# Reordering the borders of a two-pass gated-experts kernel: turnings and row loads ahead in the first unit, forms of the second pass made early, results copied out by ScalarE, residual rows loaded ahead

## The chip, the cores and the metric

The kernel runs on one core of one Trainium2 chip. The metric is device time in microseconds (us) of one execution; smaller is better. A core has TensorE (PE, with its weight loads as PEld), VectorE (DVE), ScalarE (ACT), GpSimd (POOL) and SyncE (SP), which issues nearly all DMAs here.

## The reference

Nine gated feed-forward networks (eight experts and a shared one) run on every token, their outputs are weighted and summed, and the input is added. The arrays are `x` (8, 512, 256), the gates (8, 8), the shared gate (8), and per network two weights of 256 x 1024 and one of 1024 x 256, all float32.

```python
g = einsum('bsd,edf->ebsf', h, Wg)
u = einsum('bsd,edf->ebsf', h, Wu)
expert_outs = einsum('ebsf,efd->ebsd', silu(g) * u, Wd)
expert_output = einsum('be,ebsd->bsd', gating_probs, expert_outs)
shared = einsum('bsf,fd->bsd', silu(h @ Sg) * (h @ Su), Sd)
sg = shared_gate_prob[:, :, None]
x + (1.0 - sg) * expert_output + sg * shared
```

## The kernel before

**Passes and units.** The eight batch rows are worked in two passes of four (`NH` = 2, `NI` = 4). In a pass, each of the nine networks is worked in two groups of 512 of its 1024 columns, so a pass has 18 units and the kernel 36. The last unit of a pass `closes` it, the first one `opens` it.

**Fewer products.** A unit needs the product of four weight blocks with four batch rows, for the gate (m = 0) and the up projection (m = 1). It doesn't compute all of them plainly. With a number `CI[i]` per row (0, 1, -1, 2), the two halves of a turned row and of a weight block are combined: `P_step` and `Q_step` make the four products of a block with its own row, and for each of six pairs (i, j) `R1_step` multiplies a difference of weights U by a difference of rows V and `R_step` sums of weights W by sums of rows b. `P_step` reads the half `xhub[h, i][:, 0]`, `Q_step` the half `[:, 1]`. Every product streams 512 columns.

**Forms of the rows.** For a pair, V (one 128 x 512 tile) and b (two of them) depend on the pass alone. In the unit that opens a pass they are computed, V by VectorE (`x_difference`, L169, with a ScalarE multiply L171 where needed), b by VectorE (L183) and GpSimd (L184), and stored to a DRAM scratch `xs` (L188, L189). The other 17 units load them from there (L173, L191).

**Turnings.** `turn_x` loads a batch row in two DMAs (`load_rows`), turns it with TensorE transposes (L128), and copies the two halves out by ScalarE (L150) and VectorE (L152, L154). In the first unit this happens between the products; for the second pass it happens in the last unit of the first.

**Weights.** `load_w` loads a block's weights in two DMAs (L226), `make_at` combines them by GpSimd, and for `CI` = 2 with a ScalarE multiply first (L243, L244). The next unit's weights are loaded in the steps of pairs 2 to 5.

**Down projection.** `down` multiplies the unit before by its third weight, seven products of two for each of two row pairs, into two PSUM banks `po0` and `po1` that take turns. Sums that persist over a pass are in `acc`. In the last unit of a pass the results are finished, and `ends` lists the blocks to be written.

**Results.** `turn_back` loads the residual rows `xr` (L441), turns the block into a PSUM bank (L128, named `pto`), adds with VectorE from PSUM (L448), and stores to `out` (L449). In the first unit of pass two it takes the next `po` bank, and `turned` notes that this bank is not seeded afterwards. At the end of the kernel it takes a gate bank.

**Order.** TensorE and GpSimd keep the program's order (`manual_schedule`); the instructions of VectorE, ScalarE and SP are ordered by the scheduler of the framework, by their place in the program among those that it reckons ready. A tile's buffer comes free after its last use; a tile that finds no free buffer of its tag makes its writer wait. The string `ORDER` mixes the steps of `gate_up` (G) with those of `down` (D). In unit 0, D stands for two turnings of `turn_x`; in other units for a `turn_back`, if one is listed, and a step of `down`.

## Time and profile before

| what | us |
|---|---|
| three runs | 2537.35, 2539.17, 2541.19 |
| median | 2539.17 |
| the profiled execution | 2537.59 |
| its span, first to last instruction | 2535.6 |

The span is what the profile shows; the execution's own time holds about 2 us more around it. Busy time is the union of an engine's records. A TensorE record lasts longer than the distance to the next (0.59 against 0.43 us), so TensorE's pace is read from the starts of its matmuls. A logical float32 product appears as two matmuls of 128 x 512, a transposition of one 128 x 512 half as four of 128 x 128. Unit 0 takes the time to about 70 us, and the first unit of pass two begins near 1240 us.

### The profile page before, as it was taken

Reading aid. Unit: us, or ns where it says so; the run is one execution under the profiler, and the core shown is the slowest. Engines: PE = TensorE matmul, PEld = TensorE weight load, DVE = VectorE, ACT = ScalarE, POOL = GpSimd, SP = SyncE. Lnnn points to the kernel's source line nnn. Section 1 sums busy time; section 2 is a strip of 40 time slices with the busy share of each in tenths; the row PEclk is TensorE's granted clock in tenths of the full one; section 3 lists DMA queues with packets and bytes.
Section 4 is the critical chain, followed back from the end, with each engine's and each line's share of the span. In section 5 each row is a group of like instructions: output and inputs, shape, how many; then the busy total and the mean of one; then the engine's idle time right before and its main releaser. Section 6 shows DMA issues by size and latency. Waiting matters only on the chain.

```text
span 2535.6 us, 22085 instructions
## 1 busy us (share of the span) xinstructions
PE 2502.4 (99%) x5896; PEld 1110.6 (44%) x5896; DVE 1499.3 (59%) x2267; ACT 1140.2 (45%) x2072; POOL 1908.7 (75%) x2062
## 2 busy tenths in 40 slices
PE   8999999999999999999989999999999999999998
PEld 3444444444444444444434444444444444444443
DVE  7655555555555555555785555555555555555556
ACT  3344444444444444444323444444444444444443
POOL 6778777777777777877677777877777778777773
PEclk9999999999999999999999999999999999999999
DMA  5322323233332322323343322322323333233222
GB/s 169 97 81 92 89 92 92 87 100 96 100 93 90 100 87 81 93 88 96 108 142 103 99 88 81 90 91 91 92 87 100 96 100 92 91 99 88 82 72 79
DMA packets 179738, 240.57 MB, mean 95 GB/s; under 512 B 13728, under 2 KB 122272, under 8 KB 179616
## 3 DMA queue, kind: packets, MB, share of 16 engines
q1 hardware_dynamic: 179328, 239.13, 30.8%
q8 instruction: 49, 0.80, 0.1%
q14 instruction: 73, 0.60, 0.1%
q10 hardware_dynamic: 288, 0.04, 0.0%
HBM read 225.48 MB, written 13.63 MB: 94 GB/s over the span
## 4 chain that ended last, share of the span: by engine, by line
PE 96%; DVE 2%; DMA 1%; issue 1%; POOL 0%; ACT 0%; SPq 0%; DVEq 0%; ACTq 0%; POOLq 0%
PE po L409 33%; PE c L363 29%; PE c L353 14%; PE c L309 10%; PE c L340 10%; DMA xr<-in_x_dram 0%; DVE h L300 0%; PE ptx L128 0%; DMA out_dram<-xr 0%; DVE xr L448 0%; DVE c L358 0%; DMA xin<-in_x_dram 0%; POOL z L325 0%; DMA w<-in_L_cond_Wu_dram 0%; DVE b L183 0%
## 5 line engine op out<-in xcount | busy, mean ns | idle before, releaser
L363 PE MATMUL c<-b,wb 128*128 128x512 f32 x1728 | 816.4, 594 | 1.0 <-POOL wb L244 1.0
L325 POOL TENSOR_TENSOR z<-P,Q 128x512 f32<-128x512 f32 x432 | 542.3, 1286 | 121.8 <-DVE Q L346 75.2
L300 DVE SCALAR_TENSOR_TENSOR h<-sg,coef,c 128x512 f32<-128x512 f32 x576 | 427.2, 742 | 231.5 <-PE c L363 221.8
L424 ACT COPY acc<-po 128x512 f32<-128x512 f32 x476 | 278.3, 585 | 582.9 <-PE po L409 580.0
L294 ACT ACTIVATE sg<-c 128x512 f32<-128x512 f32 x576 | 341.9, 595 | 378.7 <-PE c L363 206.3
L363 PEld LDWEIGHTS c<-b,wb 128*128 128x128 f32 x1728 | 328.9, 191 | 412.4 <-issue 393.1
L382 POOL TENSOR_TENSOR T<-h,h 128x512 f32<-128x512 f32 x284 | 357.5, 1277 | 116.1 <-PE po L409 71.9
L409 PE MATMUL po<-T,sd 128*128 128x512 f32 x864 | 435.1, 593 | 1.7 <-DVE xr L448 1.1
L353 PE MATMUL c<-v,u 128*128 128x512 f32 x864 | 435.7, 593 | 0.9 <-DVE Q L346 0.7
L357 DVE TENSOR_TENSOR c<-z,c 128x512 f32<-128x512 f32 x288 | 200.0, 695 | 335.2 <-ACT sg L294 264.1
L382 POOL TENSOR_TENSOR T<-h,T 128x512 f32<-128x512 f32 x284 | 355.8, 1277 | 6.9 <-PE po L409 6.9
L368 DVE TENSOR_TENSOR c<-c,Q 128x512 f32<-128x512 f32 x288 | 200.5, 698 | 186.5 <-PE c L363 186.5
L244 POOL TENSOR_TENSOR wb<-wb,u 128x256 f32<-128x256 f32 x216 | 155.0, 743 | 206.7 <-ACT wb L243 206.7
L409 PE MATMUL po<-h,wd 128*128 128x512 f32 x576 | 293.7, 593 | 2.0 <-DVE xr L448 2.0
L400 ACT COPY po<-acc 128x512 f32<-128x512 f32 x464 | 273.9, 590 | 43.2 <-DVE acc L426 17.0
L309 PE MATMUL c<-x,w 128*128 128x512 f32 x576 | 279.5, 598 | 7.0 <-DVE x L154 3.2
L346 DVE TENSOR_TENSOR Q<-c,P 128x512 f32<-128x512 f32 x288 | 198.1, 688 | 112.6 <-ACT sg L294 112.3
L353 PEld LDWEIGHTS c<-v,u 128*128 128x128 f32 x864 | 164.2, 190 | 208.1 <-issue 190.1
L409 PEld LDWEIGHTS po<-T,sd 128*128 128x128 f32 x864 | 163.6, 190 | 207.1 <-issue 185.9
L313 ACT COPY P<-c 128x512 f32<-128x512 f32 x288 | 168.0, 584 | 136.8 <-PE c L309 136.7
L340 PE MATMUL c<-x,at 128*128 128x512 f32 x432 | 203.0, 592 | 0.0
L358 DVE TENSOR_TENSOR c<-c,z 128x512 f32<-128x512 f32 x288 | 199.5, 693 | 0.0
(60 smaller groups left out, 1863.7 us busy)
## 6 DMA issues: line engine op xcount, KB each, us to landing
b<-xs SPq DMA_DIRECT2D x204, 512.0 KB, 3.6
v<-xs SPq DMA_DIRECT2D x204, 256.0 KB, 2.6
w<-in_L_cond_Wg_dram SPq DMA_DIRECT2D x128, 128.0 KB, 3.4
w<-in_L_cond_Wu_dram SPq DMA_DIRECT2D x128, 128.0 KB, 3.4
wd<-in_L_cond_Wd_dram SPq DMA_DIRECT2D x64, 256.0 KB, 2.7
xs<-b SPq DMA_DIRECT2D x12, 512.0 KB, 2.8
xin<-in_x_dram SPq DMA_DIRECT2D x16, 256.0 KB, 3.9
xr<-in_x_dram SPq DMA_DIRECT2D x16, 256.0 KB, 3.2
```

Source lines behind the costliest of these rows:

```text
L294: nc.scalar.activation(s, bank, AF.Silu)
L300: ve.scalar_tensor_tensor(t, u.sg[i, j], coef[:, u.e, b : b + 1], bank, ALU.mult, ALU.mult)
L309: nc.tensor.matmul(bank, u.raw[i][:, m, 0], xhub[u.h, i][:, 0], start=True, stop=True)
L325: gp.tensor_tensor(z, u.Ps[i, m], u.Qs[o, m], ALU.add)
L340: nc.tensor.matmul(bank, u.at[i][:, m], xhub[u.h, i][:, 1], start=False, stop=True, skip_group_check=True,)
L353: nc.tensor.matmul(bank, u.U[p][:, m], u.V[p], start=True, stop=True)
L363: nc.tensor.matmul(bank, u.W[p][:, r, m], u.VB[p][:, r], start=False, stop=True, skip_group_check=True,)
L368: ve.tensor_add(bank, bank, u.Qs[j, m])
L382: eng.tensor_tensor(t, a, b, ALU.subtract)
L400: nc.scalar.copy(po, acc[J, x])
L409: nc.tensor.matmul(po, u.wd[I][x], b, start=first, stop=True, skip_group_check=not first,)
L424: nc.scalar.copy(acc[J, x], po)
```

## The change

- *Unit 0*: all rows and weights are asked for before the first turning, and `make_at` follows the first products. A turning stands one step earlier in the order (`FIRST`). For the row with `CI` = 0 the half `[:, 0]` is turned first. One tiny Silu is put ahead of all ScalarE work. Of the sums z, those of pair 0 go from VectorE to GpSimd, and the combination for `CI` = 2 is two GpSimd sums.
- *Forms of pass two*: for pairs 0, 1 and 2 they are computed and stored in the last unit of pass one (`make_forms`, at its G steps 42, 45 and 48), in tiles of the pool z. The unit that opens pass two loads these three from the scratch.
- *Stores*: where a unit computes forms, their stores are collected and issued in the step of the next pair, after the next unit's `load_w` (`store_forms`).
- *Results of pass one*: ScalarE copies the turned block from PSUM to a tile `to` (one buffer), GpSimd adds the residual rows. The residual rows of a result are loaded when the one before it is written, those of the first as `down` of the closing unit begins (`load_back`).
- *Results of pass two*: all eight residual blocks are loaded before the last `down`, six into tiles of the pool z, two into `io`. The add stays with VectorE.

```diff
--- before.py
+++ after.py
@@ -109,6 +109,7 @@
         ve.tensor_copy(coef[:, E, :], sgt)
 
     scratch = {}
+    back = {}
     xhub = {}
 
 
@@ -137,14 +138,14 @@
             rows.append(t)
         return rows
 
-    def turn_x(h, pool, tag):
-
-        rows = load_rows(pool, tag, NI * h)
+    def turn_x(h, pool, tag, loaded=None):
+
+        rows = loaded or [load_rows(pool, tag, NI * h)]
         for i in range(NI):
             xt = xpool.tile([P, 2, S], F32, tag="x", name=f"x{h}_{i}")
-            for k in (1, 0):
+            for n_, k in enumerate((0, 1) if CI[i] == 0.0 else (1, 0)):
                 pt, n = new_po(f"ptx{h}_{i}_{k}", h > 0)
-                turn(pt, [rows[t // 2][:, t % 2, ts(k, P)] for t in range(NT)])
+                turn(pt, [rows[i][t // 2][:, t % 2, ts(k, P)] for t in range(NT)])
                 turned[n] = True
                 if k == 1:
                     nc.scalar.copy(xt[:, 1], pt)
@@ -154,17 +155,33 @@
                     ve.scalar_tensor_tensor(
                         xt[:, 0], xt[:, 1], -CI[i], pt, ALU.mult, ALU.add
                     )
-                if k == 0:
+                if n_ == 1:
                     xhub[h, i] = xt
-                    if i + 1 < NI:
-                        rows = load_rows(pool, tag, NI * h + i + 1)
+                    if len(rows) < NI:
+                        rows.append(load_rows(pool, tag, NI * h + i + 1))
                 yield
+
+    def make_forms(h, p):
+
+        i, j = PAIRS[p]
+        d = CI[i] - CI[j]
+        v, b0, b1 = (
+            zpool.tile([P, S], F32, tag="z", name=f"f{k}{h}_{p}") for k in range(3)
+        )
+        ve.tensor_sub(v, xhub[h, i][:, 0], xhub[h, j][:, 0])
+        if d != 1.0:
+            nc.scalar.mul(v, v, 1.0 / d)
+        ve.tensor_add(b0, v, xhub[h, j][:, 1])
+        gp.tensor_tensor(b1, v, xhub[h, i][:, 1], ALU.add)
+        scratch[h, p] = dram.tile([P, 3, S], F32, tag=f"xs{h}_{p}", name=f"xs{h}_{p}")
+        for k, t in enumerate((v, b0, b1)):
+            nc.sync.dma_start(scratch[h, p][:, k], t)
 
     def x_difference(u, p):
 
         i, j = PAIRS[p]
         v = vpool.tile([P, S], F32, tag="v", name=f"v{u.name}_{p}")
-        if u.opens:
+        if (u.h, p) not in scratch:
             d = CI[i] - CI[j]
             ve.tensor_sub(v, xhub[u.h, i][:, 0], xhub[u.h, j][:, 0])
             if d != 1.0:
@@ -179,17 +196,22 @@
         i, j = PAIRS[p]
         v = u.V[p]
         b = bpool.tile([P, 2, S], F32, tag="b", name=f"b{u.name}_{p}")
-        if u.opens:
+        if (u.h, p) not in scratch:
             ve.tensor_add(b[:, 0], v, xhub[u.h, j][:, 1])
             gp.tensor_tensor(b[:, 1], v, xhub[u.h, i][:, 1], ALU.add)
             scratch[u.h, p] = dram.tile(
                 [P, 3, S], F32, tag=f"xs{u.h}_{p}", name=f"xs{u.h}_{p}"
             )
-            nc.sync.dma_start(scratch[u.h, p][:, 0], v)
-            nc.sync.dma_start(scratch[u.h, p][:, 1:3], b)
+            u.store.append((scratch[u.h, p], v, b))
         else:
             nc.sync.dma_start(b, scratch[u.h, p][:, 1:3])
         u.VB[p] = b
+
+    def store_forms(u):
+        for to, v, b in u.store:
+            nc.sync.dma_start(to[:, 0], v)
+            nc.sync.dma_start(to[:, 1:3], b)
+        u.store = []
 
     def touch_banks():
 
@@ -198,8 +220,10 @@
             for pool, tag, n in ((ps_g, "g0", 3), (ps_g, "g1", 3), (ps_o, "po0", 1), (ps_o, "po1", 1))
             for k in range(n)
         ]
-        zero = const.tile([P, S], mybir.dt.bfloat16, name="zero")
+        zero = zpool.tile([P, 2 * S], mybir.dt.bfloat16, tag="z", name="zero")[:, :S]
         ve.memset(zero, 0.0)
+        warm = const.tile([P, 1], F32, name="warm")
+        nc.scalar.activation(warm, ident[:, 0:1], AF.Silu)
         for bank in banks:
             nc.tensor.matmul(bank, zero[:, 0:P], zero, start=True, stop=True)
 
@@ -217,7 +241,7 @@
                 u.name = f"{h}_{e}_{g}"
                 u.raw, u.at, u.U, u.W, u.V, u.VB = {}, {}, {}, {}, {}, {}
                 u.Ps, u.Qs, u.z, u.bank, u.h_ = {}, {}, {}, {}, {}
-                u.wd, u.T, u.sg = {}, {}, {}
+                u.wd, u.T, u.sg, u.store = {}, {}, {}, []
                 units.append(u)
 
     def load_w(u, i):
@@ -249,6 +273,11 @@
             u.at[i] = raw[:, :, 1]
             return
         t = atpool.tile([P, 2, P], F32, tag="at", name=f"at{u.name}_{i}")
+        if u.n == 0 and CI[i] == 2.0:
+            gp.tensor_tensor(t, raw[:, :, 0], raw[:, :, 1], ALU.add)
+            gp.tensor_tensor(t, t, raw[:, :, 0], ALU.add)
+            u.at[i] = t
+            return
         scaled_sum(t, CI[i], raw[:, :, 0], raw[:, :, 1], False)
         u.at[i] = t
 
@@ -315,7 +344,7 @@
         for p in range(ZBANK):
             a, b = PAIRS[p]
             if max(a, b) == i:
-                new_z(u, p, m, i, bank)
+                new_z(u, p, m, i, bank if u.n or p else None)
 
     def new_z(u, p, m, i, bank=None):
 
@@ -433,20 +462,39 @@
                     r, c, i = {2: (0, 0, 2), 3: (0, 1, 3), 7: (1, 1, 5), 4: (1, 0, 4)}[x]
                     ends.append((u.h, J, r, c, acc[J, i]))
 
+    BACK = [(J, r, c) for J in range(2) for r, c in ((0, 0), (0, 1), (1, 1), (1, 0))]
+
+    def block_of(a, b, r):
+        return a[b].rearrange("(p t) d -> p t d", t=NT)[:, :, ts(r, P)]
+
+    def load_back(h, J, r, c, pool=None, tag="io"):
+        if (h, J, r, c) not in back:
+            b = NI * h + 2 * J + c
+            xr = (pool or iopool).tile([P, NT, P], F32, tag=tag, name=f"xr{b}_{r}")
+            nc.sync.dma_start(xr, block_of(x, b, r))
+            back[h, J, r, c] = xr
+        return back[h, J, r, c]
+
     def turn_back(h, J, r, c, block):
 
         b = NI * h + 2 * J + c
-        rows = [a[b].rearrange("(p t) d -> p t d", t=NT)[:, :, ts(r, P)] for a in (x, out)]
-        xr = iopool.tile([P, NT, P], F32, tag="io", name=f"xr{b}_{r}")
-        nc.sync.dma_start(xr, rows[0])
+        xr = load_back(h, J, r, c)
         if h + 1 < NH:
             pt, n = new_po(f"pto{b}_{r}", True)
             turned[n] = True
         else:
             pt = ps_g.tile([P, S], F32, tag=f"g{r}", name=f"pto{b}_{r}")
         turn(pt, [block[:, ts(t, P)] for t in range(NT)])
-        ve.tensor_add(xr, pt.rearrange("p (t d) -> p t d", t=NT), xr)
-        nc.sync.dma_start(rows[1], xr)
+        if h + 1 < NH:
+            t = iopool.tile([P, S], F32, tag="to", name=f"to{b}_{r}", bufs=1)
+            nc.scalar.copy(t, pt)
+            gp.tensor_tensor(xr, t.rearrange("p (t d) -> p t d", t=NT), xr, ALU.add)
+        else:
+            ve.tensor_add(xr, pt.rearrange("p (t d) -> p t d", t=NT), xr)
+        nc.sync.dma_start(block_of(out, b, r), xr)
+        n = BACK.index((J, r, c)) + 1
+        if h + 1 < NH and n < len(BACK):
+            load_back(h, *BACK[n])
 
     def gate_up(u, nxt):
 
@@ -490,6 +538,7 @@
                 if p >= 2:
                     load_w(nxt, p - 2)
                     make_at(nxt, p - 2)
+            store_forms(u)
             for m in range(2):
                 if not last:
                     R1_step(u, p + 1, m)
@@ -510,21 +559,23 @@
     HUB = "GGDGGDGGGGDGGGGDGGDDGGDD"
     BLOCKS = ("GDGGDGGGD", "GDGGDGGGD", "GDGGDGDGGD", "GDGGDGGGD", "GDGGDGGGD", "GDGGDGDGGD")
     ORDER = HUB + "".join(BLOCKS)
+    FIRST = "DGGDGGDGG" + "G" * 46
 
 
     ends = []
     with tc.manual_schedule(engines={mybir.EngineType.PE, mybir.EngineType.Pool}):
         touch_banks()
-        turning = turn_x(0, tpool, "t")
-        next(turning)
-        load_w(units[0], 0)
-        make_at(units[0], 0)
-        next(turning)
-        for i in range(1, NI):
+        loaded = []
+        for i in range(NI):
+            loaded.append(load_rows(tpool, "t", i))
             load_w(units[0], i)
-            make_at(units[0], i)
+        turning = turn_x(0, tpool, "t", loaded)
+        for _ in range(2):
+            next(turning)
         for m in range(2):
             P_step(units[0], 0, m)
+        for i in range(NI):
+            make_at(units[0], i)
         make_coef()
         behind, acc = iter(()), {}
         for u in units:
@@ -532,7 +583,7 @@
             nxt = units[u.n + 1] if u.n + 1 < len(units) else None
             g = gate_up(u, nxt)
             nG = 0
-            for what in ORDER:
+            for what in ORDER if u.n else FIRST:
                 if what == "G":
                     if nG == 4 and u.n:
                         for _ in behind:
@@ -542,11 +593,15 @@
                         if pv.opens:
                             acc = {}
                         behind = down(pv, acc, pv.closes)
+                        if pv.closes:
+                            load_back(pv.h, *BACK[0])
                     if final and nxt is not None:
                         if nG == 18:
                             turning = turn_x(u.h + 1, iopool, "io")
                         if nG >= 18 and nG % 3 == 0:
                             next(turning, None)
+                        if nG in (42, 45, 48):
+                            make_forms(u.h + 1, nG // 3 - 14)
                     next(g)
                     nG += 1
                     if nxt is None and nG in (18, 24, 30, 36, 42):
@@ -567,6 +622,8 @@
         pv = units[-1]
         load_d(pv, (1,))
         step, due = 0, []
+        for n, at in enumerate(BACK):
+            load_back(NH - 1, *at, *((zpool, "z") if n < 6 else (iopool, "io")))
         for _ in down(pv, acc, True):
             step += 1
             if due and due[0] < step:
```

## The prediction

> **What bounds the kernel now.** I read the page first, then busy time by stage, then TensorE's waits, then the order of instructions around each wait.
>
> ```profile
> span 2535.6 us, 22085 instructions
> ...
> PE 2502.4 (99%) x5896; PEld 1110.6 (44%) x5896; DVE 1499.3 (59%) x2267; ACT 1140.2 (45%) x2072; POOL 1908.7 (75%) x2062
> ```
>
> TensorE is the bound, but 99% flatters it, since records overlap. In the 1,000 us from 1400 on, 2,331 matmuls give 0.429 us each; all 5,760 of that size need 2,471 us and the 128 transposes (four in 0.43 us) 14. Of the span about 50 us is therefore not matmul work, and all that can be won lies there.
>
> ```profile
> core 0: us, PE busy (x) PEld busy (x) DVE busy (x) ACT busy (x) POOL busy (x), PEclk, DMA share, GB/s
> 0.00:30.00 30.00, 23.83 (x69) 11.16 (x70) 15.28 (x33) 11.15 (x18) 13.22 (x20) 1.00 0.61 194
> 30.00:62.00 32.00, 29.77 (x68) 12.30 (x66) 29.29 (x41) 9.56 (x19) 29.29 (x27) 1.00 0.41 140
> 62.00:70.00 8.00, 5.20 (x9) 2.44 (x10) 5.71 (x10) 1.98 (x5) 5.99 (x9) 0.79 0.58 199
> 1255.00:1278.00 23.00, 23.00 (x61) 10.51 (x60) 18.19 (x24) 7.47 (x14) 23.00 (x19) 1.00 0.24 81
> 1278.00:1300.00 22.00, 16.10 (x38) 6.90 (x37) 16.73 (x22) 3.02 (x6) 18.14 (x17) 0.84 0.34 107
> ...
> 1100.00:1169.00 69.00, 69.00 (x162) 30.54 (x161) 39.94 (x61) 32.82 (x60) 52.91 (x59) 1.00 0.30 92
> ...
> 2526.00:2536.00 10.00, 0.00 (x0) 0.00 (x0) 1.38 (x2) 0.00 (x0) 0.00 (x0) 0.64 0.34 93
> ```
>
> The columns are length, busy time (count) per engine, then granted clock, DMA share, GB/s. The middle of a pass (1100:1169) is full. The gaps are in the first unit (30:62: VectorE 29.29 and GpSimd 29.29 of 32 us; 62:70 at clock 0.79), in the first unit of pass two (1278:1300: 16.10 of 22 us at clock 0.84, and just before it GpSimd at 23.00 of 23.00) and after the last transpose. The waits:
>
> ```profile
> PE po L409 <- DVE xr L448: 9.6, 4, 4.8
> PE c L309 <- DVE x L154: 3.2, 2, 2.0
> PE c L309 <- ACT sg L294: 3.1, 1, 3.1
> ```
>
> I set each row's start beside count times 0.429 us. Up to 30 us TensorE loses after its first product 0.37 + 2.21 + 1.30 us beside small change; from 30 to 60 us 2.6; then this:
>
> ```profile
> 59.82 1.88 PE L363 MATMUL c<-b,wb 128*128 128x512 f32 x4
> 64.80 2.07 PE L309 MATMUL c<-x,w 128*128 128x512 f32 x2 [3.10 <-ACT sg L294]
> ...
> 1278.75 1.02 PE L353 MATMUL c<-v,u 128*128 128x512 f32 x2
> 1284.58 2.05 PE L409 MATMUL po<-T,wd 128*128 128x512 f32 x2 [4.81 <-DVE xr L448]
> ```
>
> The first pair: four products need 1.72 us, so TensorE stands for 3.26 us, and the next rows at half clock cost 1.01 + 0.55. Total 4.82. The second pair: 4.97 of standing, 0.98 + 1.66 of half clock; with later waits of the same name (1.25, 1.78, 2.20) and 0.3 of small change behind them 13.1 us in all.
>
> **The change, part by part.** All sums are against the profiled execution (2537.59 us: span 2535.6 and 2.0 around it), which lies 1.6 under the median of 2539.17; the difference is taken over to the median.
>
> *(1) First turnings.* The half that `P_step` reads is now turned and copied first: ScalarE's copy of the first half starts at 7.21, VectorE's of the second at 8.06, so the first product can start 0.8 us earlier. Turning 1 moves ahead of Q0, 2 ahead of P1, 3 ahead of P2. From turning to finished operand takes 2.0 us (turned by 15.7, VectorE done at 17.7); Q0 (four products, 1.72) and the next turning (0.87) now cover it, so 2.21 and 1.30 go. No TensorE instruction is added. Loads: all eight row and eight weight DMAs go on SP's queue together, about 0.47 us of issue each. Row set 3 needs a buffer of set 0 (turned by 8.04), and weight 3 queues behind it. At the 310 GB/s of 5:10, 3 MB are in by about 12 us; weight 3 lands about 1 us later than now, and GpSimd's `make_at(3)` (two adds of 0.72 in place of ScalarE's multiply and one add) ends near 14.5 instead of 12.86. GpSimd was idle for 5.7 us before 26.01, which hides this and the two sums of 1.28 that `new_z` moves to it; without that cover they cost 4.
>
> *The activation table.* The second load goes:
>
> ```profile
> 13.23 1.28 ACT L294 ACT_TABLE_LOAD   x1
> ...
> 63.36 0.42 ACT L243 ACTIVATE at<-w 128x256 f32<-128x256 f32 x1 [5.99 <-DMA w<-in_L_cond_Wu_dram]
> 63.68 1.06 ACT L294 ACTIVATE sg<-c 128x512 f32<-128x512 f32 x2
> ```
>
> The copy before it ends at 13.21, the first Silu starts at 14.52: 1.3 us. [...]
>
> What of this reaches the end? VectorE is busy almost without a break from 15.15 to 59, so the opening cannot be shortened by more than VectorE is. It starts 1.25 earlier, has two sums less (1.3), and the 1.1 us it idled for ScalarE's copies before the old sums goes: 3.65. Bounds: 1.5 (GpSimd takes the lead) to 6 (the first four products took 3.79 us in place of 1.72, at half clock; an earlier start may end that sooner).
>
> *(2) Stores after loads.* Stores of v and b are issued by `store_forms`, after `load_w`:
>
> ```profile
> 57.37 0.42 SPq L189 DMA_DIRECT2D xs<-b  x1
> ...
> 59.15 0.52 SPq L226 DMA_DIRECT2D w<-in_L_cond_Wu_dram  x1
> ```
>
> The store at 57.37 waits for GpSimd's b, and the weight load at 59.15 stands behind it and the v load. ScalarE waits for this weight at 63.36, two activations queue behind (fence above), and TensorE behind them. The weight's buffer is free after ScalarE's multiply at 57.37; issued then, it is done issuing at 58.3, lands at 61.7 (3.4 us is the median), and TensorE goes on near 63.0 instead of 64.80, 1.5 us after its last product and without half clock. Gain 3.3. Between 0 (SP's order is a scheduler's, stores may stay ahead) and 4.8. Late next: v's buffers, held until the store; the store takes 2.0 us to land and a pair lasts 8, so nothing.
>
> *(3) Forms of pass two early.* For three pairs six VectorE operations, one ScalarE multiply, three GpSimd adds (3.8 us) and nine stores (three more than for these pairs now, 0.33 each on SP) move to the end of pass one. GpSimd idles there 7.0 + 2.5 + 1.3 us between 1218 and 1238; cost 0, without that cover 3.8. In return, SP fetches v and b for these pairs (two loads each), as in every other unit. GpSimd's two adds at 1246 and its 4.0 us wait at 1252 for a weight, whose DMA stood behind the stores of b, should go: it starts its long run about 2 us earlier.
>
> *(4) Results.* Eight VectorE adds (0.68) become eight ScalarE copies (0.59, the row of L424) and eight GpSimd adds (1.28, the row of L325). The bank is freed by the copy. In 1278:1300 ScalarE is busy 3.02 of 22 us, while VectorE reached the add for the transposes of 1277.40 only at 1283.76. So the 13.1 us lose their cause. But GpSimd gets 8 x 1.28 = 10.2 us and loses 3.8; a middle unit has 52.91 of 69. I followed its queue: its run ended in a middle unit 38.9 us after the unit's first difference; here the third form's chain, two result adds and one b come to it, some 2 us of stretching beside VectorE too, so that the second result's add ends near 1286.6. `to` has one buffer: the third copy (transposes at 1282.2 without the old stalls) waits behind that add, and TensorE needs the bank at 1284.3. That is a new stall of 0 to 5 us; I take 2.5. Gain 10.6, bounds 7 and 13. Behind a waiting copy stand ScalarE's activations, behind a waiting add GpSimd's sums. Each residual load is issued one result ahead (3.2 us to land, results 4.7 us apart or more), so the add should rarely wait for it.
>
> [...]
>
> *(5) Last results.* All eight residual blocks are loaded before the last `down`.
>
> ```profile
> 2531.34 0.69 DVE L448 TENSOR_TENSOR xr<-pto,xr 128x512 f32<-128x512 f32 x1 [4.06 <-DMA xr<-in_x_dram]
> 2532.06 0.53 SPq L449 DMA_DIRECT2D out_dram<-xr  x1
> ```
>
> The last transposes end at 2525.5. With the block there, the add runs at 2525.55 instead of 2531.34: 5.8 us. TensorE's wait of 1.1 at 2517 (VectorE stood 1.63 for a block) goes too. Eight loads (2 MB, 0.55 us of SP each) run beside matmuls with the DMAs at 0.31. Gain 6.9, bounds 5 and 8.
>
> Sum: 3.65 + 3.3 + 10.6 + 6.9 = 24.5 us; 2539.2 - 24.5 = 2514.7.
>
> **The rivals.** *GpSimd takes over in pass two's first unit*: only half of part 4 comes (5), total 19, 2520. For it: 23.00 of 23.00. Against: three idle stretches of 2.4, 5.8 and 4.3 us behind it. *It doesn't do what it says at the opening*: VectorE and GpSimd stay the pace and SP keeps stores ahead; 1.5 + 0 + 10.6 + 6.9 = 19, also 2520. *Slower*: the single `to` buffer and GpSimd's program order close a ring (copy waits for add, add for block, block for the store of two results ago, store for add). It decides once GpSimd lags more than the 4.7 us between results; my count has it at about 4.4 at one result. If it held at all seven results that follow the first, each with 3.5 us of standing and 1.7 of half clock, 36 us are lost. Against them stand 3.65 + 3.3 + 6.9 and the 13.1 of old stalls, 27: 9 slower, 2548. From six such stalls on (31) the change loses; two or three only make the gain smaller.
>
> **How the numbers follow.** My forecast 0.58, each of the first two rivals 0.16, the ring 0.06, gains that cancel 0.04. About 0.2% (5 us) can be told from no change: faster 0.90, same 0.04, slower 0.06. The bounds give 13.5 to 32 us, so 2507 to 2526; with the rivals 2506 to 2528.
>
> **What would show it.** First product near 8.0; one table load; no 3 us gap near 60; in 1255:1300 clock 1.00, no TensorE wait on a result's add but perhaps one on L424-like copies; the last store within 2 us of the last transpose. A GpSimd wait for a residual block, or half clock after 1280, would make it wrong.

## The result: 2526.43 us, half of the forecast gain

The changed kernel takes 2526.43 us (median of five, 2525.01 to 2526.94) against 2539.17. The ratio is 0.9948, with an interval of 0.9933 to 0.9962: 12.7 us are gained of the 24.5 that the sum had. The profiled spans tell the same, 2535.6 and 2523.2. From the page of the changed kernel, the span and the busy times:

```profile
span 2523.2 us, 22099 instructions
...
PE 2499.9 (99%) x5896; PEld 1108.5 (44%) x5896; DVE 1495.5 (59%) x2257; ACT 1143.4 (45%) x2079; POOL 1927.0 (76%) x2073
```

TensorE's idle time fell from 33 us to 23 (span less busy time; the page rounds both to 99%), and GpSimd has 18 us more work than before. The same stretches as before, of the changed kernel (length, busy time and count by engine, granted clock, DMA share, GB/s):

```profile
core 0: us, PE busy (x) PEld busy (x) DVE busy (x) ACT busy (x) POOL busy (x), PEclk, DMA share, GB/s
0.00:30.00 30.00, 24.68 (x79) 11.62 (x80) 19.91 (x38) 11.23 (x19) 19.26 (x25) 1.00 0.65 213
30.00:62.00 32.00, 27.25 (x59) 11.22 (x57) 24.37 (x35) 9.15 (x19) 28.65 (x28) 0.95 0.44 152
62.00:70.00 8.00, 7.45 (x17) 3.25 (x18) 8.00 (x14) 2.97 (x5) 7.76 (x12) 1.00 0.32 93
1255.00:1278.00 23.00, 23.00 (x60) 10.46 (x59) 18.14 (x25) 8.16 (x15) 21.80 (x19) 1.00 0.25 81
1278.00:1300.00 22.00, 17.68 (x45) 7.80 (x44) 13.85 (x21) 5.87 (x11) 20.11 (x18) 0.92 0.36 114
...
2526.00:2536.00 10.00, 0.00 (x0) 0.00 (x0) 0.00 (x0) 0.00 (x0) 0.00 (x0) 1.00 0.00 0
```

30:62, which had 29.77 us of TensorE, has 27.25: a wait has come in there. 62:70 has filled, 5.20 to 7.45. 1278:1300 went from 16.10 to 17.68 only. 2526:2536, where before waited for a transfer and an add, lies behind the end of the span. TensorE's longest waits in the changed kernel:

```profile
PE po L438 <- ACT to L490: 4.4, 2, 3.6
PE c L392 <- POOL wb L268: 3.4, 1, 3.4
PE po L438 <- ACT po L429: 2.6, 2, 2.2
...
PE c L338 <- ACT sg L323: 1.4, 1, 1.4
```

Of the three rows shown of before, VectorE's add is gone and the wait for a Silu has fallen from 3.1 to 1.4. Three new names stand ahead of it. The line numbers have moved: L438 is `down`'s product (L409 before), L392 `R_step` (L363), L338 `P_step` (L309), L369 `Q_step` (L340), L490 and L491 are the new copy and the new add of a result, L178 the store of an early form. TensorE's timeline of the changed kernel at the three places where it stands longest (start, duration, instruction, idle time before it):

```profile
44.56 1.02 PE L382 MATMUL c<-v,u 128*128 128x512 f32 x2
48.93 3.07 PE L392 MATMUL c<-b,wb 128*128 128x512 f32 x4 [3.35 <-POOL wb L268]
...
58.73 1.88 PE L392 MATMUL c<-b,wb 128*128 128x512 f32 x4
62.04 1.13 PE L338 MATMUL c<-x,w 128*128 128x512 f32 x2 [1.43 <-ACT sg L323]
...
1233.66 1.02 PE L338 MATMUL c<-x,w 128*128 128x512 f32 x2
1236.87 1.10 PE L438 MATMUL po<-T,sd 128*128 128x512 f32 x2 [2.19 <-ACT po L429]
1237.81 3.34 PE L392 MATMUL c<-b,wb 128*128 128x512 f32 x4
...
1284.74 1.02 PE L382 MATMUL c<-v,u 128*128 128x512 f32 x2
1289.38 2.08 PE L438 MATMUL po<-h,wd 128*128 128x512 f32 x2 [3.62 <-ACT to L490]
1291.25 2.60 PE L392 MATMUL c<-b,wb 128*128 128x512 f32 x4
```

Four matmuls of 0.429 us need 1.72 us, two need 0.86. From one start to the next, less that: the first place loses 3.51 in standing and, until 53.50, 1.15 + 0.84 at half clock (granted clock 0.50 in 51.97:53.50, where the starts lie 0.85 us apart in place of 0.43). The second (62.04, the old 4.82 us stall) loses 1.59, and 0.66 a little later. At 1233.66 a stall that before did not have loses 2.35, then 1.40 and 0.29 at half clock (0.50 in 1239.20:1241.00). The third result loses 3.78, then 1.01 + 0.72 (0.50 in 1289.38:1291.25). Where half clock is named below without a granted clock, it is read from this pace of the starts.

Where both kernels reach the same product, the balance reads (profiled executions, from the starts of TensorE's instructions):

| until | before | after | difference to here |
|---|---|---|---|
| R1 of pair 0 in unit 0 | 29.66 | 24.69 | -4.97 |
| the product that waits for pair 3's `wb` | 51.99 | 48.93 | -3.06 |
| first `down` product | 78.38 | 74.93 | -3.45 |
| first unit of pass two | 1241.72 | 1242.08 | +0.36 |
| behind the last result of pass one | 1344.32 | 1338.94 | -5.38 |
| end of the span | 2535.6 | 2523.2 | -12.4 |

So the opening brought 3.45 us. Up to 1242 another 0.3 was gained, and a new stall of 4.1 took all of it back. Pass two's first unit brought 5.74, the end 7.0.

### The profile page after: what moved, and what is told of

Its sections match the earlier page's. It is cut to its first block, busy times and chain, and to the rows that moved or that the text cites. A ratio compares the mean times of both kernels' runs of the same rounds, so it can differ in the third digit from the quotient of the medians.

```text
span 2523.2 us, 22099 instructions
## 1 busy us (share of the span) xinstructions
PE 2499.9 (99%) x5896; PEld 1108.5 (44%) x5896; DVE 1495.5 (59%) x2257; ACT 1143.4 (45%) x2079; POOL 1927.0 (76%) x2073
## 4 chain that ended last, share of the span: by engine, by line
PE 95%; POOL 2%; DVE 1%; issue 1%; DMA 0%; ACT 0%; ACTq 0%; SPq 0%; POOLq 0%; DVEq 0%
PE po L438 33%; PE c L392 28%; PE c L382 14%; PE c L338 10%; PE c L369 10%; POOL z L354 1%; POOL T L411 1%; DMA w<-in_L_cond_Wu_dram 0%; POOL wb L268 0%; DMA sgt<-ondB_sharedgateprob_dram 0%; PE pto L129 0%; POOL b L201 0%; POOL u L287 0%; PE ptx L129 0%; DVE v L186 0%
## 5 line engine op out<-in xcount | busy, mean ns | idle before, releaser
L392 PE MATMUL c<-b,wb 128*128 128x512 f32 x1728 | 817.4, 594 | 3.4 <-POOL wb L268 3.4
L392 PEld LDWEIGHTS c<-b,wb 128*128 128x128 f32 x1728 | 328.6, 191 | 415.5 <-issue 391.2
L438 PE MATMUL po<-T,sd 128*128 128x512 f32 x864 | 435.3, 593 | 2.6 <-ACT po L429 2.6
L438 PE MATMUL po<-h,wd 128*128 128x512 f32 x576 | 294.6, 594 | 4.4 <-ACT to L490 4.4
L429 ACT COPY po<-acc 128x512 f32<-128x512 f32 x464 | 273.7, 590 | 36.2 <-DVE acc L455 14.3
L338 PE MATMUL c<-x,w 128*128 128x512 f32 x576 | 276.5, 593 | 2.8 <-ACT sg L323 1.4
L438 PEld LDWEIGHTS po<-T,sd 128*128 128x128 f32 x864 | 163.7, 190 | 208.5 <-issue 188.5
L369 PE MATMUL c<-x,at 128*128 128x512 f32 x432 | 203.1, 592 | 1.5 <-DVE z L356 1.5
```

The costliest lines, as they stand in the source:

```text
L338: nc.tensor.matmul(bank, u.raw[i][:, m, 0], xhub[u.h, i][:, 0], start=True, stop=True)
L369: nc.tensor.matmul(bank, u.at[i][:, m], xhub[u.h, i][:, 1], start=False, stop=True, skip_group_check=True,)
L392: nc.tensor.matmul(bank, u.W[p][:, r, m], u.VB[p][:, r], start=False, stop=True, skip_group_check=True,)
L429: nc.scalar.copy(po, acc[J, x])
L438: nc.tensor.matmul(po, u.wd[I][x], b, start=first, stop=True, skip_group_check=not first,)
```

## The experiments

Each was measured beside the kernel before, whose median lay between 2537.74 and 2539.17 in the four sets of measurements. So a gain is given twice where it matters: as the distance to the changed kernel's 2526.43, and as what it is beside its own runs of before, where the changed kernel has 12.7. Differences of less than about 1.5 us between two experiments are not told apart here.

**The end alone.** The kernel before, with only the residual loads ahead of the last `down`:

```diff
+        for n, (J, r, c) in enumerate(order):
+            pool, tag = (zpool, "z") if n < 6 else (iopool, "io")
+            xr = pool.tile([P, NT, P], F32, tag=tag, ...)
+            nc.sync.dma_start(xr, ...)
+            back[NH - 1, J, r, c] = xr
         for _ in down(pv, acc, True):
```

> Kernel before with one edit: the eight residual blocks of pass two are loaded before the last `down`, as in the change. Theory A (the end is a part by itself): 7 us under the kernel before, about 2532, the last store 1 us after the last transpose. Rival B (part of the gain at the end is owed to what precedes it): less than 5 us.

2531.71 us (2530.07 to 2532.57), ratio 0.9971 (0.9960 to 0.9983), 7 us below its runs of before (2538.58). Part 5 stands as it was forecast. In the changed kernel the last add of VectorE reads thus, where before it had an idle time of 4.06 us for a block:

```profile
2518.22 0.66 PE L129 MATMUL pto<-ident,acc 128*128 128x128 f32 x4 [0.42 <-DVE acc L455]
2518.91 0.69 DVE L493 TENSOR_TENSOR xr<-pto,xr 128x512 f32<-128x512 f32 x1 [0.15 <-PE pto L129]
```

It starts 0.69 us after the start of the last transposes (2518.22), as they end. What follows it is the store alone, as before.

**The opening alone.** The changed kernel with the old `turn_back`, without `load_back` and without early forms. Unit 0 differs from before, and little else (the stores of pass two's forms are collected too):

```diff
-                        if pv.closes:
-                            load_back(pv.h, *BACK[0])
-                        if nG in (42, 45, 48):
+                        if False:
                             make_forms(u.h + 1, nG // 3 - 14)
-        for n, at in enumerate(BACK):
-            load_back(NH - 1, *at, ...)
```

> Of the change only what concerns unit 0: early loads and turnings, the early Silu, two z and the factor 2 on GpSimd, stores after the loads. Forms and both kinds of results as in the kernel before. Theory A (the opening gives what the two traces differ by at the first down product, 3.5 us): 2534.5. Theory B (the prediction's 7 us, with the rest lost later to what the earlier start meets): 2531 or below.

2534.38 us (eleven runs, 2532.67 to 2536.61), ratio 0.9981 (0.9972 to 0.9990): 4.8 us below its runs of before (2539.15). The interval, 2.5 to 7.1 us, does not by itself rule out the 6.95 of parts 1 and 2; the profile speaks against it: the first `down` product starts at 75.45, 2.9 us earlier than before, and the old end-of-unit stall is nearly whole: 2.79 of standing and 1.01 + 0.75 at half clock, 4.55 against 4.82, although its stores too are collected.

**Are the stores what held the loads?** The changed kernel with the stores where the forms are made, as before:

```diff
-            u.store.append((scratch[u.h, p], v, b))
+            nc.sync.dma_start(scratch[u.h, p][:, 0], v)
+            nc.sync.dma_start(scratch[u.h, p][:, 1:3], b)
```

> Changed kernel with one edit: the stores of v and b stand in the program where the forms are made, as in the kernel before. Theory A (their place decides how late the last weight load of unit 0 goes out): the wait before the next unit's first product, 1.6 us now, grows to 3 us or more, with half clock behind it; 2 to 3 us over the changed kernel, 2529. Rival B (SP's order comes out much the same, and the gain there was the earlier opening): within 1 us of 2526.

2525.16 us (2524.04 to 2529.61), ratio 0.9952 (0.9939 to 0.9966). The median does not differ. Part 2 wanted the store of pair 4's b (57.37 before) behind the weight load at 59.15. GpSimd's half of that b in the kernel before, then the same store and the same load on SyncE's queue in the changed kernel, then both in this one:

```profile
53.26 1.73 POOL L184 TENSOR_TENSOR b<-v,x 128x512 f32<-128x512 f32 x1
```

```profile
54.30 0.42 SPq L213 DMA_DIRECT2D xs<-b  x1
...
56.44 0.50 SPq L250 DMA_DIRECT2D w<-in_L_cond_Wu_dram  x1
```

```profile
54.48 0.42 SPq L206 DMA_DIRECT2D xs<-b  x1
...
56.21 0.49 SPq L251 DMA_DIRECT2D w<-in_L_cond_Wu_dram  x1
```

The store stands ahead of the load in all three kernels. By the program, too, `store_forms` issues it behind the load of the next unit's second block, and the load that ScalarE waits for is that of the fourth. So part 2's lever did not act. Nor did the store hold the load before: its data was there at 54.99 (53.26 + 1.73). TensorE stands 4.10 us at the end of unit 0 in this profile, with the weights issued no later than in the changed kernel. Two of the five times are higher than the rest (2528.78 and 2529.61, the profiled one); whether the stores make such executions more frequent, five of them can't tell.

**Then what holds the end of unit 0?** ScalarE in the changed kernel, the multiply for `CI` = 2 and two Silus that TensorE needs:

```profile
60.60 0.42 ACT L267 ACTIVATE at<-w 128x256 f32<-128x256 f32 x1 [4.32 <-DMA w<-in_L_cond_Wu_dram]
60.92 1.07 ACT L323 ACTIVATE sg<-c 128x512 f32<-128x512 f32 x2
```

The multiply starts when the weight has landed, and the Silus are queued behind it. TensorE's first product of the next unit starts 1.44 us after the multiply in each of the nine profiles that keep the multiply on ScalarE (60.60 and 62.04 here, 63.36 and 64.80 before, 60.23 and 61.67 in the opening alone, 61.47 and 62.91 with the stores as before). The experiment takes only this multiply off ScalarE in unit 1 (GpSimd makes the combination with two sums, as in unit 0):

```diff
-        if u.n == 0 and CI[i] == 2.0:
+        if u.n <= 1 and CI[i] == 2.0:
```

> Changed kernel with one edit: the combination of the weights with factor 2 is two GpSimd sums in unit 1 too, so that ScalarE's activations no longer stand behind a multiply that waits for a weight's DMA. Theory A (ScalarE's order holds TensorE at the end of unit 0): the wait of 1.4 us near 61 goes; about 2 us under the changed kernel, 2524.5. Rival B (the same wait moves to GpSimd, whose sums T and differences U stand behind it): within 1 us of 2526.

2522.21 us (2521.15 to 2523.21), ratio 0.9939 (0.9926 to 0.9951), 4.2 us less than the changed kernel (15.5 beside its runs of before, 2.8 more). The two Silus, and the old stall on TensorE's timeline of this kernel:

```profile
57.49 1.20 ACT L323 ACTIVATE sg<-c 128x512 f32<-128x512 f32 x2 [2.84 <-DVE c L397]
```

```profile
58.83 1.04 PE L338 MATMUL c<-x,w 128*128 128x512 f32 x2
59.70 1.88 PE L392 MATMUL c<-b,wb 128*128 128x512 f32 x4
61.98 1.13 PE L338 MATMUL c<-x,w 128*128 128x512 f32 x2 [0.39 <-DVE h L329]
```

The product at 58.83 is the one that starts at 62.04 in the changed kernel, and it follows its predecessor without a stand: the 1.59 is gone. What is lost up to 61.98, 0.56, is the later 0.66. The holder was ScalarE's own order: Silus whose inputs were there stood behind a multiply whose weight was not. The first `down` product starts at 71.52 instead of 74.93. About 1.7 of these 3.4 us are the stall, the rest is half clock at 50 us, which this execution did not have. But that rest is not luck: four other profiles had no half clock there either and keep the multiply, and TensorE, sooner at the end of unit 0, then stood 2.72 to 4.26 us for it. In all seven profiles with the new opening and the multiply the first `down` product starts between 74.56 and 76.73, in the four without the multiply between 70.42 and 71.63.

**GpSimd or VectorE in unit 0?** The change gave GpSimd the sums z of pair 0. This gives them back:

```diff
-                new_z(u, p, m, i, bank if u.n or p else None)
+                new_z(u, p, m, i, bank)
```

> Changed kernel with one edit: in unit 0 the two sums z of pair 0 are again made by VectorE. Theory A (GpSimd's queue, full from 12 to 54 us, paces the first unit): the weight sums reach TensorE 2 to 2.5 us sooner, the wait of 3.4 us near 46 shrinks to about 1 and the half clock after it goes; 3 to 5 us under the changed kernel, about 2522. Rival B (VectorE paces it, as the prediction had it): 1 us or more later, 2527 or above.

2524.85 us (2523.09 to 2528.21), ratio 0.9949 (0.9936 to 0.9961): not different, and between the two theories. TensorE's waits on its timeline:

```profile
29.78 2.04 PE L382 MATMUL c<-v,u 128*128 128x512 f32 x2 [3.16 <-DVE Q L375]
...
49.46 1.99 PE L392 MATMUL c<-b,wb 128*128 128x512 f32 x4 [1.04 <-POOL wb L268]
```

The wait for GpSimd's `wb` falls from 3.35 to 1.04, but the product starts at 49.46, not before 48.93. VectorE has it now: 3.16 us for Q at 29.78. In the changed kernel GpSimd runs up to that point almost without a break:

```profile
11.64 0.73 POOL L265 TENSOR_TENSOR at<-w 128x256 f32<-128x256 f32 x1 [1.31 <-DMA w<-in_L_cond_Wu_dram]
12.67 0.83 POOL L277 TENSOR_TENSOR at<-w 128x256 f32<-128x256 f32 x1 [0.30 <-DMA w<-in_L_cond_Wu_dram]
...
41.52 5.46 POOL L354 TENSOR_TENSOR z<-P,Q 128x512 f32<-128x512 f32 x4
46.92 1.27 POOL L201 TENSOR_TENSOR b<-v,x 128x512 f32<-128x512 f32 x1
48.14 1.87 POOL L268 TENSOR_TENSOR wb<-wb,u 128x256 f32<-128x256 f32 x2
```

Its first sum starts at 9.60; from 12.67 on it has no idle time up to the `wb` sums. In the ten profiles with the new opening and either share of z the product that waits for `wb` starts between 48.93 and 50.31 us, though TensorE's first four matmuls took between 1.82 and 3.58 us in them (with half of z moved, in a further experiment below, it starts at 48.18). So both engines are full in unit 0; what the share of z changes (48.93 and 49.46) is less than the spread of these profiles.

**The copy's buffer.** The copy goes into the tile of the block just transposed, which needs no further buffer:

```diff
-            t = iopool.tile([P, S], F32, tag="to", ..., bufs=1)
-            nc.scalar.copy(t, pt)
-            gp.tensor_tensor(xr, t.rearrange(...), xr, ALU.add)
+            nc.scalar.copy(block, pt)
+            gp.tensor_tensor(xr, block.rearrange(...), xr, ALU.add)
```

> Changed kernel with one edit: ScalarE copies a turned result into the block's own tile (dead once it is turned), so no copy waits for the add before it. Theory A (the single buffer `to` is what holds TensorE): the wait of 3.6 us near 1285 and its half clock go, also the one of 0.7 near 1329; 6 us under the changed kernel, about 2520.5. Rival B (GpSimd's lag itself holds TensorE, the buffer only shows it): the stall moves to another wait on GpSimd (a sum z or wb) in 1280:1300, and the time stays within 2 us of 2526.

2522.60 us (2520.95 to 2523.97), ratio 0.9934 (0.9921 to 0.9948), 3.9 us less (16.0 beside its runs of before, 3.2 more). The chain in the changed kernel, on GpSimd and on ScalarE: the second result's add, then the third copy, which waits for it.

```profile
1287.45 1.26 POOL L491 TENSOR_TENSOR xr<-to,xr 128x512 f32<-128x512 f32 x1
```

```profile
1288.74 0.59 ACT L490 COPY to<-pto 128x512 f32<-128x512 f32 x1 [5.42 <-POOL xr L491]
```

And the stretch with the buffer taken away:

```profile
core 0: us, PE busy (x) PEld busy (x) DVE busy (x) ACT busy (x) POOL busy (x), PEclk, DMA share, GB/s
1255.00:1300.00 45.00, 44.37 (x116) 20.19 (x115) 36.86 (x50) 15.87 (x30) 43.80 (x38) 1.00 0.29 92
```

TensorE goes from 40.69 us in this stretch (changed kernel) to 44.37, at full clock. The stall is gone; 1.55 us of it come back at 1308.84, where the next unit's Silu is late. It goes with a gain of 3.9 in place of 6.

**The early forms, left out.**

```diff
-                        if nG in (42, 45, 48):
+                        if False:
```

> Changed kernel without `make_forms`: the unit that opens pass two computes all six pairs' forms itself, as in the kernel before. Theory A (making forms early costs its stall of 4 us near 1234 and brings little): 2 to 4 us under the changed kernel, 2523 or 2524, with no wait near 1234 and the stall at the third result not much longer. Rival B (the forms relieve GpSimd in pass two's first unit, as the prediction had it, by 2 us of its queue and one sum): the waits in 1255:1300 grow by 3 us or more beside the 4 that go, 2526 or above.

2526.57 us (2524.61 to 2526.80), ratio 0.9955 (0.9942 to 0.9967): the same as the changed kernel (11.2 beside its runs of before). The stall at 1234 is not there. But the third copy, in this kernel:

```profile
1287.75 0.58 ACT L490 COPY to<-pto 128x512 f32<-128x512 f32 x1 [7.79 <-POOL xr L491]
```

```profile
1288.39 2.08 PE L438 MATMUL po<-h,wd 128*128 128x512 f32 x2 [6.07 <-ACT to L490]
```

It waits 7.79 us instead of 5.42, and TensorE stands 6.23 us (from start to start) instead of 3.78, with 1.15 at the second result. Without early forms the profile is 4.1 us shorter between the first `down` product and the first unit of pass two (1163.01 against 1167.15), and 4.2 longer from there to behind the last result (101.04 against 96.86): they are worth some 4 us and cost some 4 us.

**The early forms' stores, behind the last weight load.** They keep their place in the computation; only the nine stores move to G steps 47 and 50:

```diff
-        for k, t in enumerate((v, b0, b1)):
-            nc.sync.dma_start(scratch[h, p][:, k], t)
+        made.append((scratch[h, p], (v, b0, b1)))
...
+                        if nG in (47, 50):
+                            store_made()
```

> Changed kernel with one edit: the forms of pass two are computed where they were, but their stores stand in the program behind the next unit's last weight load (G steps 47 and 50). Theory A (the stores of forms stand on SP's queue between the two halves of a weight load, wait for GpSimd, and hold ScalarE and then TensorE): the wait of 2.2 us near 1234 and its half clock go, 4 us in all; about 2522.5. Rival B (the added work of VectorE, ScalarE and GpSimd there holds TensorE): the wait stays, within 1 us of 2526.

2522.56 us (2522.45 to 2523.42), ratio 0.9937 (0.9925 to 0.9950), 3.9 us less (16.0 beside its runs of before, 3.3 more). SyncE's queue in the changed kernel, ScalarE behind it, and then SyncE's queue in the experiment:

```profile
1221.54 0.42 SPq L250 DMA_DIRECT2D w<-in_L_cond_Wg_dram  x1
1228.39 4.45 SPq L178 DMA_DIRECT2D xs<-f  x4
1232.89 0.43 SPq L250 DMA_DIRECT2D w<-in_L_cond_Wu_dram  x1
```

```profile
1235.22 0.42 ACT L267 ACTIVATE at<-w 128x256 f32<-128x256 f32 x1 [7.29 <-DMA w<-in_L_cond_Wu_dram]
```

```profile
1221.98 0.42 SPq L257 DMA_DIRECT2D w<-in_L_cond_Wg_dram  x1
1222.46 0.46 SPq L257 DMA_DIRECT2D w<-in_L_cond_Wu_dram  x1
1228.83 4.46 SPq L184 DMA_DIRECT2D xs<-f  x4
```

In the changed kernel the two halves of one block's weights are issued at 1221.54 and 1232.89. Between them stand four stores, the last of which waits for a form that GpSimd finishes at 1232.5 (1231.22 + 1.27). ScalarE's multiply waits 7.29 us for the second half, the seed copy that TensorE needs (L429) is behind the multiply, and TensorE stands. In the experiment the second half is issued at 1222.46, and TensorE loses 0.88 us there instead of 2.35 + 1.40 + 0.29.

**The three cures together** (own tile, late stores, the multiply off ScalarE in unit 1):

> Three edits on the changed kernel together: result copied into the block's own tile, form stores behind the weight loads, the combination with factor 2 on GpSimd in unit 1. If the three stalls are independent the gains add: 3.9 + 3.9 + 2 = 10 us under 2526.4, about 2516.6. If GpSimd's lag grows as TensorE is freed, less than 6 us, 2520 or above.

2515.80 us (four runs, 2515.49 to 2517.04), ratio 0.9915 (0.9901 to 0.9928): 10.6 us below the changed kernel, where the three alone add up to 12.0; beside the runs of before, 9.2 us where the three add up to 9.3. So the three stalls are nearly independent. This version beats both kernels. Its first unit of pass two:

```profile
1255.00:1300.00 45.00, 44.12 (x117) 19.84 (x115) 34.57 (x46) 13.10 (x27) 45.00 (x40) 1.00 0.43 138
```

TensorE has 44.12 of 45 us at full clock, beside a GpSimd without a free moment.

**Two variants of it.** First, z for m = 0 of pair 0 back to VectorE:

```diff
-                new_z(u, p, m, i, bank if u.n or p else None)
+                new_z(u, p, m, i, bank if u.n or p or m == 0 else None)
```

> e9_best with one more edit: of the two sums z of pair 0 in unit 0, the one for m = 0 goes back to VectorE, the other stays with GpSimd. Theory A (both engines pace the first unit in turn, so half of the moved work is the right share): the waits on GpSimd's weight sums (1.0) and on VectorE's z (2.0) in unit 0 shrink together, 1 to 2 us under e9_best, 2514.5. Rival B (any further shift only moves the wait to VectorE's Q): within 0.5 us of 2515.8 or above it.

2515.63 us (2514.70 to 2517.90), ratio 0.9909 (0.9894 to 0.9924): the same by the medians, 1.6 us better beside its runs of before (23.5 against 21.9), which isn't told apart. Its waits for `wb` (2.0) and Q (1.3) have taken the place of others; that halving the moved work helps is not shown. Second, own tile and the multiply off ScalarE, but no early forms at all:

> e9_best with the forms of pass two made in the opening unit (`make_forms` never called): own tile for the copy, factor 2 on GpSimd in unit 1. Theory A (early forms help only because GpSimd's lag reaches TensorE through the single buffer): within 1 us of e9_best, 2516. Rival B (GpSimd's lag holds TensorE in other ways too, through z and wb): the waits in 1255:1300 grow to 3 us or more, 2518 or above.

2518.58 us (2517.70 to 2519.76), ratio 0.9918 (0.9905 to 0.9932), 2.8 us more than the three together by the medians, 1.4 beside the runs of before (20.6 gained against 21.9), so the times alone leave it open. The profiles show both sides: without the early forms the end of pass one is 1.8 us shorter (1163.01 against 1164.78 from the first `down` product on), and the stretch from there to behind the last result 4.1 longer (97.29 against 93.16). With the buffer out of the way GpSimd's lag still reaches TensorE, as a wait of 3.8 us for a Silu near 1303. So in these two profiles the early forms are worth more than they cost, once their stores are out of the way.

## Why the prediction was right and wrong

The range held the time, 1.6 us inside its upper end; the forecast of 2514.7 lay 11.7 us too low. One of its own signs of being wrong came: half clock after 1280 (granted clock 0.92 in 1278:1300, 0.50 in 1289.38:1291.25; it had named 1.00). Its other signs came out: first product at 8.25, one table load, 1.6 us of standing in place of 3.3 near 60, a TensorE wait on the copies, no GpSimd wait for a residual block, the last store right behind the last add. By its own steps:

| step | forecast | measured | by |
|---|---|---|---|
| (1) first turnings, up to the `wb` product | 3.65 | 3.06 | balance |
| half clock behind the wait at `wb` | 0 | -2.0 | timeline |
| (2) the stall at the end of unit 0 | 3.3 | 2.4 (4.82 to 2.46) | timeline; 0.3 in the opening alone |
| (3) early forms | 0 | -4.1 before 1242; the +4 behind it is within (4) | balance; forms left out |
| (4) results | 10.6 | 5.7 | balance |
| (5) last results | 6.9 | 7.0 | balance; 7 alone |

With the 0.3 before 1242 the measured column adds up to the span's 12.4. The first three rows have to be read together, as the 3.45 us of the opening. When the next unit starts is set by the multiply on its last weight. Where there was no half clock behind `wb`, TensorE came to the end of unit 0 sooner and stood longer there: in the opening alone it arrived at 58.88 instead of 60.45 and began the next unit at 61.67 instead of 62.04.

**(5) is right**, cause and size.

**(1): nearly the size, but another engine.** The step took VectorE's occupation as the limit and gave GpSimd's idle time as the cover for what moves to it. Before, GpSimd had 8.9 us of idle time between its first sum (9.81) and 34 us. In the changed kernel it starts 0.2 earlier (9.60), waits 1.6 for weights (1.31 + 0.30), has two sums z more (2.5) and one more for the weights (0.8), and its other sums take some 1.1 longer in all (nine of them took 0.33 to 0.50 us more than the usual 0.73 or 1.27, in the kernel before six). That leaves 3.1, and it reaches the `wb` sums 3.07 earlier: GpSimd sets the pace, without any reserve. TensorE, 4.97 ahead at pair 0's R1, stands there, with 2.0 at half clock afterwards. Neither is in the sum. The wait would have been found by writing out GpSimd's queue for unit 0, as was done for pass two. That the second table load goes was right: in the changed kernel the one load is at 1.66. Its 1.3 us lie off the path that GpSimd sets.

**(2): the mechanism was wrong.** The step took the store at 57.37 for what held the weight load at 59.15. The store's data had been there since 54.99, the store stays ahead of that load in the changed kernel, and with the stores put back the median does not change; with the opening alone the stall is nearly whole. The bound of 0 was named, for a scheduler that keeps its own order, and given too little weight. The chain behind the load was read rightly (weight, multiply, Silus, TensorE), and the lever on it was one link later: not the store ahead of the load, but the multiply ahead of the Silus. What the place gained comes from the whole opening being earlier: the weight's load is issued at 56.44 in place of 59.15, and the multiply starts at 60.60 in place of 63.36. The loss there, 2.46 in one profile, 4.55 in another and 6.05 in a third, is set by two times: the multiply's start (60.60, 60.23 and 61.47) and TensorE's arrival (60.45, 58.88 and 58.65), with the half clock behind a long stand. Why a weight issued at much the same time (56.44, 56.24, 56.21) reaches the multiply after 4.0 us in one execution and after 5.3 in another stays open.

**(3): a step that moved, priced without its queue.** It counted nine stores at 0.33 us of SyncE and found cover on GpSimd. It did not ask what stands behind a store whose data is late. One did: half a weight, 11 us after the other half. The gain that the step named (GpSimd freer behind 1252) is real, though it was not put in the sum: about 4 us, found only by leaving the forms out. It is part of the 5.7 measured for step 4.

**(4): right mechanism, a term too small.** The new stall behind the single `to` was foreseen at the third result. It was taken as 2.5 us, of 0 to 5, and measured 3.78 + 1.01 + 0.72 = 5.5. The count of GpSimd's queue had the second add end near 1286.6; it ended at 1288.7 (1287.45 + 1.26). The stretching in that count shows in the trace of before: sums z took up to 1.73 us in 1246:1300, at most 1.29 in 1100:1169. And the half clock behind the stand (1.01 + 0.72), which the sum had for the old stalls, was left out for the new one. Besides, 1.9 us more of the old 13.1 were not gained: 0.85 before the third result's transposes (TensorE stood 0.69 for VectorE's last sum into the block), 0.90 at a late result, and small change. That the buffer is the cause is shown by taking it away, and so is what GpSimd's lag adds: without early forms the same stall is 6.23. The ring of the slower rival did not close: it had one such stall, not seven.

Two rivals came true in part at once: GpSimd's lead, and an opening that does not do what it says. They had been priced each alone, at 2520; both together take 5.6 and 5.45 from the sum and give 2525.7. That this is within a microsecond of the measured time is partly chance: the opening lost less than the rival had it, and the 4.1 of the early forms' stores was in none of the cases.

## What to carry to other kernels

Before work is moved to an engine with idle time, write out that engine's queue with its new start and its new sums: here 8.9 us of idle time became 1.6, all of it before 13 us. For every instruction that is added to an in-order queue, ask how long it can wait for its own input and what is ready behind it. A store of late data ahead of a load, and a multiply on a late weight ahead of ready activations, cost some 3 to 4 us each here, without any engine being busier. Before a load is moved on an in-order queue, check that what stands ahead of it has to wait at all. Price a new stall with the half clock that may follow it: here 23 of 27 stands of more than 2.2 us lost mostly 1.5 to 2.8 us more.

## What the runs showed of the hardware

- *How long a stand is followed by half clock.* In the thirteen profiles, behind 12 us, no stand of TensorE between 1 and 2.2 us was followed by more than 0.4 us lost at half clock (starts some 0.86 us apart in place of 0.43). Of the 27 longer ones 23 were, by 1.5 to 3.1 us: 2.28 by 1.80, 2.35 by 1.69, 2.79 by 1.76, 3.51 by 1.99, 3.78 by 1.73, 4.97 by 2.64. The granted clock was 0.67 in 1236.80:1242.00, behind the one of 2.35, and in the kernel before 0.50 in 64.80:66.00 and in 1284.58:1287.00, behind those of 3.26 and 4.97. But stands of 2.42, 2.87, 3.00 and 3.98 us were followed by at most 0.4, and the granted clock was 1.00 in 0:70 around the one of 3.00 (early forms left out) and in 1240:1345 around the one of 3.98 (own tile, no early forms). So the length alone does not decide; what else does, no run here shows.
- *Unit 0's first four matmuls* took 3.79 us in the kernel before, 1.82 in the changed one, and between 1.82 and 3.58 in nine experiments with the same first instructions. It differs by execution, and the product that waits for `wb` started between 48.93 and 50.31 us in all of these. Part 1 put the 3.79 us down to half clock; the granted clock in 8:12 of that trace is 1.00, while it is 0.50 with 3.58 us in the experiment on the copy's buffer. That an earlier start shortens it is not shown: in the changed kernel and the nine experiments the first of the four started between 8.20 and 8.34.
